# Attention products of two chunks in one run, and two output products in shared PSUM banks

## The chip, the cores and the metric

The kernel runs on one core of one Trainium2 chip. The metric is the device time of one execution in microseconds (us), lower is better. The engines that matter here are TensorE (PE, matrix products; its weight loads are shown as PEld), VectorE (DVE), ScalarE (ACT) and GpSimd (POOL); SyncE (SP) issues most of the transfers. Products are written into PSUM, which has eight banks of 512 float32 columns on 128 partitions; PE writes it, DVE and ACT read it.

## What is computed

One transformer block in float32: causal attention with rotary positions (4 sequences of 1024 tokens, width 256, 16 heads of 64), a residual and a layer norm, then a mixture of experts (16 experts, the best 3 for each token), a residual and a layer norm. The change lies in attention alone:

```python
proj = x @ W_in.T + b_in
...
q = _rope(q, sin, cos)
k = _rope(k, sin, cos)
att = jnp.einsum('bhqd,bhkd->bhqk', q, k) * scale
att = jnp.where(mask, att, -jnp.inf)
att = jax.nn.softmax(att, axis=-1)
y = jnp.einsum('bhqk,bhkd->bhqd', att, v)
y = y.transpose(0, 2, 1, 3).reshape(b, t, H * VD)
return y @ W_out.T + b_out
```

## The kernel before

Attention works on pairs of heads: 8 pairs for each of the 4 sequences, `n` from 0 to 31. A sequence is cut into 8 chunks of 128 tokens. Each pair is worked through in six slots, `k` from 0 to 5 (the loop from L535), and the pairs are a pipeline: while the scores of pair `n` are made, the rest of pair `n - 1` is finished and the queries and keys of pair `n + 1` are projected. The order of instructions on PE and DVE is the order in which the code stands; it is written out by hand (`manual_schedule`).

Slot by slot, on PE, for a pair `n` in the middle:

- slot 0: scores of query chunk 7; output product 3 of pair `n - 2`; a key projection; products of key chunks 4 and 3 of pair `n - 1`
- slot 1: scores of chunk 6; a key projection; products 2 and 1 of pair `n - 1`
- slot 2: scores of chunk 5; a query projection; product 0 of pair `n - 1`, then `close(n - 1)`
- slot 3: scores of chunk 4; product 7 of pair `n`; output product 0 of pair `n - 1`; a value projection
- slot 4: scores of chunks 3 and 2; product 6 of pair `n`; output product 1 of pair `n - 1`; a value projection
- slot 5: scores of chunks 1 and 0; a query projection; output product 2 of pair `n - 1`; product 5 of pair `n`

`scores` (L393) multiplies queries by keys, DVE masks and reduces the result to its row minimum (L401), ACT takes the exponential (L416), POOL divides by the row sum (L433), and two slots later DVE transposes the probabilities in 32x32 blocks into `t_last` and `t_first` (`turn`, L452).

`product(n, j)` (L459 to L485) multiplies the transposed probabilities of key chunk `j` by the values of that chunk. Chunk `j` matters to query chunks `j` to 7 alone, so low chunks have wide products. Each product has 32 rows and 64 columns of weights, so PE is cut into eight positions: four row groups `a` (0 to 3) times two column halves `hh`, one for each head. There are four products `u` for each position. Some of them are of a kind that the mask cuts by 32 columns more (`skip`): for an odd chunk those with `u < a`, for an even chunk those with `u > a`. Odd chunks have thus more work in row group 0, even ones in row group 3. In chunk 7 the cut products are empty and left out: 20 products, ordered by row group, in place of 32. All products of a pair add up in four PSUM tiles `y`, one for each row group, of which the first 256 of 512 columns are used. The pool `ps_y` has those four buffers, so product 7 of a pair can write a tile when `close` of the pair before has copied it.

`close(n)` (L487) has ACT copy the four tiles, with the bias of the values, into `yT` in SBUF. `out(n, h)` (L500) multiplies a quarter of `yT`, as weights, by the output weights (two products, L503), into a buffer of the pool `ps_s`, and DVE adds the result to the residual (L590).

The pool `ps_s` has the other four PSUM banks. The scores, projections, value products and output products take its buffers in turn; each waits until what was last in the buffer has been read by DVE or ACT.

DVE also takes router work of the batch before into its idle times (`fill`), so that later pairs have more of it than the first eight. After the last pair two more turns of the loop finish what is left, and the mixture of experts follows (L1054 to L1121).

Of the kernel before, what the change touches and what calls it, by code (L numbers as in the profile page):

```python
# [29 lines left out]
FP = mybir.dt.float32  # L30
I32 = mybir.dt.int32
AF = mybir.ActivationFunctionType
ALU = mybir.AluOpType
AX = mybir.AxisListType
PSUM = bass.MemoryType.PSUM
# [3 lines left out]
P = 128  # L39
B, T, D = 4, 1024, 256  # L40
H, KD = 16, 64
# [3 lines left out]
TC = T // P  # L45
# [74 lines left out]
def attention(  # L120
# [6 lines left out]
    nc = tc.nc  # L127
    with ExitStack() as ctx:
        def pool(name, bufs, **kw):
            return ctx.enter_context(tc.tile_pool(name=name, bufs=bufs, **kw))  # L130
# [13 lines left out]
        sp = pool("a_small", 4)  # L144

        ps_s = pool("ps_s", 4, space=PSUM)
        ps_y = pool("ps_y", 4, space=PSUM)

        xT_v = xT.rearrange("b (c p) t -> b p c t", p=P)
        x_v = x.rearrange("b (c p) d -> b p c d", p=P)  # L150
# [291 lines left out]
        turned = {}  # L442
# [11 lines left out]
                probs[n, i, hh][:, ds(512 * h, n_j * P)].rearrange("p (j u q) -> p u j q", u=4, q=32),  # L454
            ), kind)

        st = {}

        def product(n, j):  # L459


            if j == TC - 1:
                st[n] = [ps_y.tile([P, 512], FP, tag="y", name="y_ps") for _ in range(4)]
            h, jh = divmod(j, 4)
            t, c = turned[n][h], jh // 2
            v, c = (vrs[n, h, c], 0) if h else (vrs[n, h, None], c)
            at = jh * (8 - 4 * h)
            us = range(4) if 0 < j < TC - 1 else range(3, -1, -1)
            parts = [(u, hh, a) for u in us for hh in range(2) for a in range(4)]

            def whole(u, a):
                return u >= a if j % 2 else u <= a

            if j == TC - 1:

                parts = sorted((p for p in parts if whole(p[0], p[2])), key=lambda p: -min(3 - p[2], 2))
            for u, hh, a in parts:
                skip = 0 if whole(u, a) else 1
                nc.tensor.matmul(  # L479
                    st[n][a][ts(hh, KD), ds(32 * (j + skip), 32 * (TC - j - skip))],  # L480
                    lhsT=v[ts(a, 32), c * 8 + 2 * u + jh % 2, ts(hh, KD)],
                    rhs=t[ts(a, 32), hh, u, ds(at + skip, TC - j - skip), :],
                    start=(j == TC - 1 and u == 3), stop=(j == 0 and u == 0),
                    skip_group_check=True,
                )  # L485

        def close(n):  # L487
            p = n % NP
            yT = yp.tile([P, TC, 4, 32], FP, tag="yT")
            y = st.pop(n)  # L490
            for a in reversed(range(4)):

                y_copied = nc.scalar.activation(  # L493
                    yT[:, :, a, :], y[a][:, : 2 * P].rearrange("p (i q) -> p i q", q=32),
                    AF.Identity, bias=bv[:, p : p + 1],
                )
            st[n] = yT.rearrange("p i a q -> p (i a q)")
            router.closed = y_copied

        def out(n, h):  # L500
            ps = ps_s.tile([P, 2, D], FP, tag="s", name="oo")
            for v in range(2):
                nc.tensor.matmul(  # L503
                    ps[:, v, :], lhsT=st[n][:, ts(2 * h + v, P)], rhs=wo[n],
                    start=True, stop=True,
                )
            return accs[n // NP][:, ds(2 * h, 2), :D], ps

# [25 lines left out]
        with tc.manual_schedule(engines={mybir.EngineType.PE, mybir.EngineType.DVE}):  # L534
            for n in range(n_pairs + 2):  # L535
# [3 lines left out]
                for k in range(n_slots):  # L539
# [32 lines left out]
                    if k == 2 and before:  # L572
                        product(n - 1, 0)
                        close(n - 1)
                    if k in (3, 4) and here:
                        product(n, 10 - k)
                    if k in (0, 3, 4, 5) and one_of(n - 1 - (k == 0)):
                        part = out(n - 1 - (k == 0), (k - 3) % 4 if k else 3)
                    if k in (3, 5):
# [44 lines left out]
                    if k == 0 and one_of(n):  # L624
                        rotate(n, 0, 0)
                    if k < 2 and before:
                        product(n - 1, 4 - 2 * k)
                        product(n - 1, 3 - 2 * k)
                    m = n + 2 - n % 2
                    if k in (3, 4) and one_of(m):  # L630
                        values(m, 2 * (n % 2) + k - 3)
# [736 lines left out]
```

## Time and profile before

| what | value |
|---|---|
| time, median of 3 runs | 1563.44 us (1563.33 to 1567.95) |
| the profiled execution, its own time | 1566.73 us |
| its span, first to last instruction | 1565.0 us |
| mean granted TensorE clock | 0.986 |
| attention, first to last product (L479) | 40.0 to 1125.9 us |
| a pair of heads, most of them | 33.60 us |
| matmuls of `product` (L479), `t_first` and `t_last` | 8192 and 7424 |
| matmuls of `out` (L503) | 512 |
| ACT's copies in `close` (L493) | 128, median 476 ns |
| DVE's sums after `out` (L590) | 128, mean 659 ns |

A float32 product is recorded as two matmuls, each with its weight load. A line of the timeline has the start in us, the time from the first start to the last end, the engine, line, operation, what is written and read, the tile on PE, the shape and the count; idle time before it and what ended it stand in brackets. Matmuls overlap: the end of a line is modelled and lies behind the start of the next, so a step's cost is read from start to start.

### The profile page before, as it was taken

How to read it: one execution, taken by the hardware profiler on the slowest of the kernel's cores; microseconds unless marked ns; L12 is line 12 of the kernel's file. 1: busy time of each engine (PE TensorE's matmuls, PEld its weight loads, DVE VectorE, ACT ScalarE, POOL GpSimd, SP SyncE). 2: the span in 40 equal slices, each digit the busy share in tenths (PEclk: the TensorE clock that was granted, in tenths of full speed). 3: DMA queues.
4: the chain of work that ended last, by engine and by line, in shares of the span. 5: the costliest groups of instructions: out<-in, count | busy, mean ns of one | idle time of the engine just before them, and what ended most of it. 6: DMA issues, size and time to landing. Idle time of an engine off the chain costs nothing.

```text
span 1565.0 us, 52508 instructions
## 1 busy us (share of the span) xinstructions
PE 1502.5 (96%) x20844; PEld 1051.4 (67%) x20844; DVE 1173.4 (75%) x3677; ACT 730.7 (47%) x1695; POOL 979.7 (63%) x932
## 2 busy tenths in 40 slices
PE   8999999999999999999999999999899999999990
PEld 4566666666666666666665666665588888888880
DVE  4788888898899999988999999889857333333334
ACT  3555555557555555664554556654342222222224
POOL 3676565676556667776776667767457764444444
PEclk9999999999999999999999999999999999999995
DMA  6554545546454554564546445645488998888868
GB/s 187 142 151 128 147 119 138 165 119 187 110 145 120 138 160 113 155 182 135 162 134 168 125 124 144 187 127 138 151 311 259 374 307 227 257 255 258 259 131 328
DMA packets 120473, 280.34 MB, mean 179 GB/s; under 512 B 21392, under 2 KB 64656, under 8 KB 108688
## 3 DMA queue, kind: packets, MB, share of 16 engines
q1 hardware_dynamic: 100304, 250.05, 53.1%
q0 software_dynamic: 19584, 26.62, 8.1%
q8 instruction: 166, 2.72, 0.7%
q14 instruction: 83, 0.68, 0.1%
q10 hardware_dynamic: 336, 0.27, 0.1%
HBM read 186.81 MB, written 61.09 MB: 158 GB/s over the span
## 4 chain that ended last, share of the span: by engine, by line
PE 89%; DVE 6%; DMA 2%; issue 2%; ACT 1%; SPq 0%; POOL 0%; ACTq 0%; DVEq 0%; POOLq 0%
PE y_ps L479 18%; PE s L393 17%; PE pp L290 14%; PE ps L1106 11%; PE ps L1090 11%; PE oo L503 7%; PE vv L343 7%; PE ps L1054 1%; DVE p L401 1%; DVE t_first L452 1%; PE lg_ps L723 1%; DMA vr<-v_d 1%; DVE o_stats L1226 1%; DMA more<-sums 0%; PE x_ps L715 0%
## 5 line engine op out<-in xcount | busy, mean ns | idle before, releaser
L433 POOL TENSOR_SCALAR p<-p,rinv 128x512 f32<-128x512 f32 (+7 forms) x512 | 374.8, 747 | 340.6 <-DVE rinv L430 310.3
L416 ACT ACTIVATE p<-p,nmax 128x512 f32<-128x512 f32 (+7 forms) x512 | 391.7, 766 | 412.6 <-DVE nmax L401 322.4
L393 PE MATMUL s<-rotk,rotq 64*128 64x512 f32 (+3 forms) x1536 | 310.9, 514 | 4.0 <-DVE rotk L326 2.7
L452 DVE STREAM_TRANSPOSE t_first<-p 128x512 f32<-128x512 f32 (+3 forms) x512 | 275.9, 582 | 8.6 <-PE y_ps L479 8.4
L1121 POOL DMA_INDIRECT sums<-y,ids x104 | 163.1, 1569 | 162.1 <-DVE y L1117 126.3
L290 PE MATMUL pp<-xT,wqk 128*128 128x512 f32 x512 | 250.9, 613 | 3.0 <-DVE nmax L401 3.0
L1095 ACT ACTIVATE hid<-ps,w 128x256 f32<-128x256 f32 (+1 forms) x224 | 89.7, 456 | 289.8 <-issue 237.7
L479 PE MATMUL y_ps<-t_first,vr 32*64 32x224 f32 (+3 forms) x8192 | 208.7, 331 | 6.9 <-issue 2.7
L393 PEld LDWEIGHTS s<-rotk,rotq 64*128 64x128 f32 x1536 | 139.0, 187 | 100.8 <-issue 56.5
L479 PEld LDWEIGHTS y_ps<-t_first,vr 32*64 32x64 f32 x8192 | 168.9, 131 | 55.4 <-issue 47.5
L1111 DVE TENSOR_TENSOR y<-ps,w 128x512 f32<-128x512 f32 (+1 forms) x56 | 36.6, 653 | 215.8 <-PE ps L1106 192.5
L1090 PE MATMUL ps<-xg,w 128*128 128x256 f32 (+1 forms) x896 | 189.5, 364 | 1.3 <-DVE xg L1057 0.7
L1106 PE MATMUL ps<-w,hid 128*128 128x256 f32 x832 | 188.8, 379 | 0.5 <-ACT hid L1095 0.5
L401 DVE CUSTOM_DVE_ANT_0 p<-s,zero_and_mask,nmax 128x512 f32<-128x512 f32 x256 | 181.8, 748 | 2.9 <-PE s L393 0.7
L401 DVE CUSTOM_DVE_ANT_0 p<-s,mask 128x512 f32<-128x512 f32 (+1 forms) x256 | 131.8, 552 | 62.9 <-PE s L393 62.8
L1106 PEld LDWEIGHTS ps<-w,hid 128*128 128x128 f32 x832 | 157.2, 190 | 21.6 <-ACT hid L1095 0.7
L290 PEld LDWEIGHTS pp<-xT,wqk 128*128 128x128 f32 x512 | 89.9, 190 | 119.7 <-issue 63.2
L1090 PEld LDWEIGHTS ps<-xg,w 128*128 128x128 f32 x896 | 157.2, 190 | 19.2 <-DVE xg L1057 1.0
L479 PEld LDWEIGHTS y_ps<-t_last,vr 32*64 32x64 f32 x7424 | 104.9, 131 | 76.5 <-issue 49.8
L503 PE MATMUL oo<-wo,yT 128*128 128x256 f32 x512 | 141.0, 398 | 2.9 <-ACT yT L493 1.6
L479 PE MATMUL y_ps<-t_last,vr 32*64 32x32 f32 (+3 forms) x7424 | 126.8, 243 | 0.5 <-DVE t_last L452 0.4
L820 POOL DMA_INDIRECT xs<-acc,slots x96 | 97.3, 1014 | 44.3 <-issue 21.2
(190 smaller groups left out, 1833.9 us busy)
## 6 DMA issues: line engine op xcount, KB each, us to landing
w<-in_wall_dram SPq DMA_DIRECT2D x56, 1154.0 KB
vr<-v_d SPq DMA_DIRECT2D x256, 128.0 KB
vr<-v_d SPq DMA_DIRECT2D x128, 256.0 KB
swq<-rawq SPq DMA_DIRECT2D x256, 64.0 KB
v_d<-v SPq DMA_DIRECT2D x128, 128.0 KB
swk<-rawk SPq DMA_DIRECT2D x124, 128.0 KB
x<-xs SPq DMA_DIRECT2D x48, 264.0 KB
wqk<-in_w_qk_dram SPq DMA_DIRECT2D x32, 256.0 KB
```

Of the source, the lines that this page charges most:

```text
L290: nc.tensor.matmul(ps, lhsT=wqk[n][:, c, i, :], rhs=xts[b, g][:, c, :], start=(c == 0), stop=(c == DC - 1),)
L343: nc.tensor.matmul(ps[:, u, :], lhsT=xts[b, cc // 2][:, c, ts(cc % 2 * 2 + u, P)], rhs=wv[n][:, c, :], start=(c == 0), stop=(c == DC - 1),)
L393: nc.tensor.matmul(s[:, :n_k], lhsT=rot[n, 0, qc // 4][ts(hh, KD), ts(qc % 4, P)], rhs=k[ts(hh, KD), ds(k0, n_k)], start=True, stop=True,)
L401: i = nc.vector.tensor_tensor_reduce(out=probs[n, qc, hh][:, ds(k0, n_k)], in0=s[:, :n_k], in1=masks[qc % 2][:, 512 - n_k :] if diag else ...
L416: order["exp"] = nc.scalar.activation(pr, pr, AF.Exp, bias=m, scale=-1.0, accum_out=rsum[:, hh : hh + 1])
L433: order["divide"] = router.behind = nc.gpsimd.tensor_scalar(pr, pr, rinv[:, hh : hh + 1], 1.0, ALU.mult, ALU.mult)
L452: order["turn"] = router.on_dve = after(nc.vector.transpose(turned[n][h][:, hh, :, ds(i - 4 * h, n_j, step=7 - 4 * h), :], probs[n, i, hh] ...
L479: nc.tensor.matmul(st[n][a][ts(hh, KD), ds(32 * (j + skip), 32 * (TC - j - skip))], lhsT=v[ts(a, 32), c * 8 + 2 * u + jh % 2, ts(hh, KD)], ...
L503: nc.tensor.matmul(ps[:, v, :], lhsT=st[n][:, ts(2 * h + v, P)], rhs=wo[n], start=True, stop=True,)
L1090: nc.tensor.matmul(ps[:, f - f0, :], lhsT=w[:, ds(c * FF + f * P, P)], rhs=xg[:, c, :n], start=(c == 0), stop=(c == DC - 1),)
L1106: nc.tensor.matmul(ps[:, h, :], lhsT=hid[:, f, ts(h, P)], rhs=w[:, ds(W2_AT + f * D, D)], start=(f == 0), stop=(f == FC - 1),)
L1121: s = behind(nc.gpsimd.indirect_dma_start(out=sums_of(t), out_offset=bass.IndirectOffsetOnAxis(ap=ids[:, h : h + 1], axis=0), in_=y[:, h, ...
```

## The change

Four things change.

1. The four PSUM tiles of `product` become one tile of four banks, `[P, 4, 512]`, in a pool with one buffer. Product 7 of a pair therefore starts when everything that reads the tile of the pair before is done.
2. `product` takes several chunks at once and puts their products into one order: each position's products are numbered by the columns that the position has been sent before, and all are sorted by that number. Chunks 7 and 6 are now one such run in slot 4 (slot 3 has no product any more), 4 and 3 are one in slot 0, 2 and 1 one in slot 1. Chunks 5 and 0 stay alone, but are sorted too.
3. Output products 0 and 1 go into the unused columns 256 to 511 of the banks of the product tile: output 0 of pair `n - 1` into banks 0 and 1 of its own tile, in slot 3, output 1 of pair `n - 1` into banks 2 and 3 of the tile of pair `n`, in slot 4 after the run of chunks 7 and 6. They are written without the flag that begins an accumulation (`start=False`). Outputs 2 and 3 stay in `ps_s`.
4. In the last pair two of the four copies of `close` are made by DVE.

```diff
-        ps_y = pool("ps_y", 4, space=PSUM)
+        ps_y = pool("ps_y", 1, space=PSUM)
...
+        def product(n, *js):
+
+            if js[0] == TC - 1:
+                st[n] = banks["y"] = ps_y.tile([P, 4, 512], FP, tag="y", name="y_ps")
+            todo, moved = [], {}
+            for j in js:
+                first_last = j in (0, TC - 1)
+                for u in range(3, -1, -1) if first_last else range(4):
+                    for hh in range(2):
+                        for a in range(4):
+                            skip = u < a if j % 2 else u > a
+                            if skip and j == TC - 1:
+                                continue
+                            at = moved.get((hh, a), 0)
+                            moved[hh, a] = at + TC - j - skip
+                            todo.append((at if j < TC - 1 else -min(3 - a, 2), j, u, hh, a, int(skip)))
+            for _, j, u, hh, a, skip in sorted(todo, key=lambda i: i[0]):
...
                 nc.tensor.matmul(
-                    st[n][a][ts(hh, KD), ds(32 * (j + skip), 32 * (TC - j - skip))],
+                    st[n][ts(hh, KD), a, ds(32 * (j + skip), 32 * (TC - j - skip))],
...
+                from_y = y[:, a, : 2 * P].rearrange("p (i q) -> p i q", q=32)
+                if n == n_pairs - 1 and a % 2:
+                    nc.vector.tensor_scalar(
+                        yT[:, :, a, :], from_y, bv[:, p : p + 1], 1.0, ALU.add, ALU.mult
+                    )
+                else:
+                    y_copied = nc.scalar.activation(
+                        yT[:, :, a, :], from_y, AF.Identity, bias=bv[:, p : p + 1],
+                    )
...
         def out(n, h):
-            ps = ps_s.tile([P, 2, D], FP, tag="s", name="oo")
+            apart = h == 0 or (h == 1 and n + 1 < n_pairs)
+            if apart:
+                ps = banks["y"][:, ds(2 * h, 2), D:]
+            else:
+                ps = ps_s.tile([P, 2, D], FP, tag="s", name="oo")
             for v in range(2):
                 nc.tensor.matmul(
                     ps[:, v, :], lhsT=st[n][:, ts(2 * h + v, P)], rhs=wo[n],
-                    start=True, stop=True,
+                    start=not apart, stop=True, skip_group_check=apart,
                 )
...
-                    if k in (3, 4) and here:
-                        product(n, 10 - k)
+                    if k == 4 and here:
+                        product(n, 7, 6)
...
                     if k < 2 and before:
-                        product(n - 1, 4 - 2 * k)
-                        product(n - 1, 3 - 2 * k)
+                        product(n - 1, 4 - 2 * k, 3 - 2 * k)
```

More of the change, by code (lines that the diff above doesn't have):

```diff
@@ L455, in turn @@
             ), kind)
[L457 to L478, printed above, removed]
+        st, banks = {}, {}
@@ new lines, in product @@
+        def product(n, *js):
[14 more added lines that the diff above has]
+            for _, j, u, hh, a, skip in sorted(todo, key=lambda i: i[0]):
+                h, jh = divmod(j, 4)
+                t, c = turned[n][h], jh // 2
+                v, c = (vrs[n, h, c], 0) if h else (vrs[n, h, None], c)
@@ L479, in product @@
                 nc.tensor.matmul(
-                    st[n][a][ts(hh, KD), ds(32 * (j + skip), 32 * (TC - j - skip))],
+                    st[n][ts(hh, KD), a, ds(32 * (j + skip), 32 * (TC - j - skip))],
                     lhsT=v[ts(a, 32), c * 8 + 2 * u + jh % 2, ts(hh, KD)],
-                    rhs=t[ts(a, 32), hh, u, ds(at + skip, TC - j - skip), :],
+                    rhs=t[ts(a, 32), hh, u, ds(jh * (8 - 4 * h) + skip, TC - j - skip), :],
                     start=(j == TC - 1 and u == 3), stop=(j == 0 and u == 0),
@@ L491, in close @@
             for a in reversed(range(4)):
[L493 to L496, printed above, removed]
+                from_y = y[:, a, : 2 * P].rearrange("p (i q) -> p i q", q=32)
[7 more added lines that the diff above has]
+                    )
             st[n] = yT.rearrange("p i a q -> p (i a q)")
```

## The prediction

> **What bounds the kernel now.** I read the page first. TensorE (PE) has work in flight for 96% of the span, and nine tenths of the chain that ended last are PE.
>
> ```profile
> PE 1502.5 (96%) x20844; PEld 1051.4 (67%) x20844; DVE 1173.4 (75%) x3677; ACT 730.7 (47%) x1695; POOL 979.7 (63%) x932
> ...
> PE 89%; DVE 6%; DMA 2%; issue 2%; ACT 1%; SPq 0%; POOL 0%; ACTq 0%; DVEq 0%; POOLq 0%
> ...
> L503 PE MATMUL oo<-wo,yT 128*128 128x256 f32 x512 | 141.0, 398 | 2.9 <-ACT yT L493 1.6 <-DVE nmax L401 1.0
> ```
>
> So only what shortens PE's own row of work counts. The output products (L503) lose 2.9 us in all to waits: there is next to nothing to win by giving them other buffers.
>
> Then the timeline of PE over one pair of heads (start, duration, engine, line). A step's cost is the start of the next line minus its own.
>
> ```profile
> 174.27 1.45 PE L393 MATMUL s<-rotk,rotq 64*128 64x128 f32 x8
> 175.65 0.73 PE L479 MATMUL y_ps<-t_last,vr 32*64 32x32 f32 x40
> 176.31 1.13 PE L503 MATMUL oo<-wo,yT 128*128 128x256 f32 x4
> 177.28 1.89 PE L343 MATMUL vv<-wv,xT 128*128 128x256 f32 x8
> 179.10 1.77 PE L393 MATMUL s<-rotk,rotq 64*128 64x512 f32 x8
> 180.80 0.93 PE L479 MATMUL y_ps<-t_last,vr 32*64 32x64 f32 x64
> 181.66 1.13 PE L503 MATMUL oo<-wo,yT 128*128 128x256 f32 x4
> ...
> 188.08 1.05 PE L479 MATMUL y_ps<-t_last,vr 32*64 32x96 f32 x64
> 189.05 1.99 PE L393 MATMUL s<-rotk,rotq 64*128 64x512 f32 x8
> ...
> 199.60 2.97 PE L479 MATMUL y_ps<-t_first,vr 32*64 32x192 f32 x128
> 202.50 1.56 PE L393 MATMUL s<-rotk,rotq 64*128 64x256 f32 x8
> 203.99 1.98 PE L290 MATMUL pp<-xT,wqk 128*128 128x512 f32 x4
> 205.91 1.98 PE L479 MATMUL y_ps<-t_first,vr 32*64 32x224 f32 x64
> ```
>
> Chunk 7's product costs 0.66 (slot 3), chunk 6's 0.86 here and 0.90 in most pairs (slot 4), chunk 5's 0.97, 4 with 3 2.18 (193.80 to 195.99 of the same timeline), 2 with 1 2.90, chunk 0's 1.91. Such a pair lasts 33.60 us, and most of the 31 do: VectorE (DVE) is busy for 87% of it in the first batch and up to 96% later, which PE hides.
>
> The next timeline shows what chunk 7's product hides in slot 3 of the following pair.
>
> ```profile
> 207.82 1.45 PE L393 MATMUL s<-rotk,rotq 64*128 64x128 f32 x8
> 208.00 1.56 ACT L493 ACTIVATE yT<-y_ps,bv 128x256 f32<-128x256 f32 x4
> 209.20 0.73 PE L479 MATMUL y_ps<-t_last,vr 32*64 32x32 f32 x40
> 209.86 1.13 PE L503 MATMUL oo<-wo,yT 128*128 128x256 f32 x4
> ```
>
> The output product needs all four copies of yT, which end at 209.56. PE spends the time till then on the scores and on chunk 7.
>
> **Slot 3 loses chunk 7's product.** Its output product would follow the scores at 209.20, but waits for yT: 209.56 + 0.05 (at the end of attention yT ends at 1127.51 and the output starts at 1127.56) = 209.61 in place of 209.86. Of the 0.66 us that leave, 0.25 are won; the other 0.41 had been free cover. Bounds: 0.66 if the copies came sooner, 0 if the output came no sooner; both ends of the wait are rows, so I take -0.25.
>
> **Slot 4 gets 52 products for 32.** No row has the merged run. The nearest is chunk 6's, whose 0.86 us I cut into windows (start:end, length, then busy time and count of what is in work, matmuls first, weight loads second):
>
> ```profile
> 180.80:181.08 0.28, 0.28 (x32) 0.28 (x33) 1.00 0.26 69
> 181.08:181.15 0.07, 0.07 (x31) 0.07 (x12) 1.00 0.12 29
> 181.15:181.48 0.33, 0.33 (x51) 0.33 (x33) 1.00 0.29 31
> 181.48:181.66 0.18, 0.18 (x24) 0.11 (x9) 1.00 0.10 28
> ```
>
> The first 16 products (32 matmuls, a product being two) are issued within 0.28 us, the other 16 in the next 0.40, and the last 0.18 passes to the next step with few loads left. After the first 16 a product costs 0.40/16 = 25 ns: 0.28 + 36 x 0.025 + 0.18 = 1.36 us. Below: all at the first pace, 0.28/16 = 17.5 ns, gives 1.09. Above: the two rows' sum, 0.66 + 0.90 = 1.56. I take 1.36, against 0.90 so far: +0.46 (+0.19 to +0.66).
>
> **The order inside the runs.** PE has eight positions (four row groups by two column halves). Before, each round of eight gives the odd chunks' extra 32 columns to one group and the even chunks' to another; now a product goes where the fewest columns have been sent. Chunk 0's run shows what a column costs where nothing is uneven: its busiest position takes 4 products of 256 columns, 32 blocks of 32. A block is 0.053 us: in the run of chunks 4 and 3 a position's 128-column matmuls, each half of four blocks, follow each other by 0.107 us. So 32 are 1.71 of its 1.91: entry and exit are 0.20. Chunks 4 and 3 give each position 33 blocks: 1.76 + 0.20 = 1.96 against 2.18; 2 and 1 give 49: 2.61 + 0.20 = 2.81 against 2.90. At most 0.22 + 0.09 = 0.31 is there; nothing at all if PE's queue already evens it out. Wide blocks (2, 1) are near chunk 0's row, so most of 0.09; narrow ones (4, 3) are nearer to chunk 5's, whose 12 blocks should take 0.84 and take 0.97 for want of issue: I take half of each, -0.15. Chunks 5 and 0 keep their heaviest position: 0, within 0.03.
>
> **The banks.** The outputs of slots 3 and 4 no longer take a buffer from the scores' four; that wait was 26.8 us of idle weight loads but 1.0 of matmuls: 0. In return PE gets waits. The merged run's first matmul now waits for the sum of slot 3 (DVE, old L590), and behind it in PE's queue stand the whole run, an output and a value projection, for which ACT's copy waits. In the timeline of DVE that sum ends at 179.09, the run's place is 180.80: 1.7 us to spare (1.57 at the least in full pairs). Chunk 5's product waits for the sum of slot 4, which ends at 183.78, against 188.08. Cost 0; beyond that slack each us late is lost in each pair. The sums stay where they are in DVE's order, no DMA and no step of POOL moves.
>
> [...] If each of the two waits exposed its sum of 0.65 us, 24 pairs would lose 31 us; by the slack above they lose none. [...]
>
> **The last close** is split between ACT and DVE: four copies took 1.57 us at 1125.94 with nothing beside them. Two take about half, and DVE, which idles then, does the others: -0.7 (0 to -0.8).
>
> **The sum.** A pair changes by -0.25 + 0.46 - 0.15 = +0.06. Six pairs (from 515, 550, 652, 826, 930 and 965 us on) wait for DVE in slots 1 and 2, together some 7 us over 2.90 and 1.49, and swallow either sign; the last pair is DVE's too. So 24 x 0.06 = +1.4; the first pair has no output in slot 3: 1.36 for 0.62 + 0.84, -0.1; the end -0.7. Total +0.6. The profiled execution took 1566.7 around a span of 1565.0, the median of the runs is 1563.4; on that median I predict **1564.0 us**.
>
> **Rivals.** About 0.3% (4.7 us) is what a measurement of this kernel tells from no change; below, "same" means within it.
> - *Slower: the merged run is no cheaper than its two rows.* It is long enough to live on the slow pace, and nothing but its own rate sets it. For: chunk 6's row falls from 17.5 to 25 ns a product after 16. Against: one entry and exit are saved. At 1.56 the pair changes by +0.26: 24 x 0.26 - 0.8 = +5.4, 1568.9; if the order also brings nothing, +0.41 x 24 - 0.8 = +9, 1572.5. With the order's 0.15 it decides from 1.53 us a run.
> - *Faster: evenness was the limit.* Both sorted runs fall to their columns and the merged one keeps the first pace: -0.25 + 0.19 - 0.31 = -0.37, 24 times and -0.8: 1553.8. For: 0.22 of excess in chunks 4 and 3. Against: chunk 5's excess, which no order removes. Half of it gives 1558.2, about the border.
> - *It frees buffers, and that is what counts:* the 7 us in the six pairs go, 1557. Against: those waits are two slots away from the outputs that move, for turns and reductions of DVE, whose work stays.
> - *It doesn't do what it says:* the runs stay apart. The built order shows 52 products in one run, so no chance.
>
> **How the numbers follow.** Forecast 0.55, own range 1559 to 1568. Slower 0.25, faster by evenness 0.15, by buffers 0.05. Range with both sides, cut where 0.2 is left out: **1555 to 1571**. Faster 0.20, same 0.55, slower 0.25.
>
> **What would show it.** Slot 3's output starts at yT's end + 0.05, some 0.4 us after the scores would let it; the merged run of 104 matmuls lasts 1.36; 4 with 3 falls to about 2.07, 2 with 1 to 2.85; a full pair lasts 33.5 to 33.8; the end of attention has two copies a side. I am wrong if the merged run starts late (the sum of DVE), if it is under 1.2 or over 1.5, or if pairs that wait for DVE change.

## The result, and the profile after

The changed kernel takes 1568.96 us (median of 20 runs, 1565.89 to 1572.57), the kernel before, run beside it, 1564.48 us (20 runs, 1562.27 to 1567.95): ratio 1.0028, 95% interval 1.0021 to 1.0035. It is slower by about 4.5 us, just inside the 0.3% that the prediction counted as no change; 1564.0 had been forecast, with a range of 1555 to 1571.

The page of the changed kernel begins as that of before, but its chain of work that ended last is another:

```profile
PE 1491.7 (95%) x20844; PEld 1045.0 (67%) x20844; DVE 1175.4 (75%) x3679; ACT 730.0 (47%) x1693; POOL 979.8 (63%) x932
...
PE 75%; DVE 11%; ACT 5%; issue 4%; DMA 3%; SPq 1%; POOL 1%; ACTq 0%; POOLq 0%; DVEq 0%
```

PE is busy for 10.8 us less (1502.5 before), and yet the span is longer: what was saved on PE came back as waiting. The chain, nine tenths PE before, now leaves it in every pair. The timeline of PE over one pair shows where (start, duration, engine, line, operation; idle time before it and what ended it in brackets; start to start is a step's cost):

```profile
203.94 1.45 PE L393 MATMUL s<-rotk,rotq 64*128 64x128 f32 x8
205.73 1.13 PE L512 MATMUL y_ps<-wo,yT 128*128 128x256 f32 x4 [0.34 <-ACT yT L499]
206.70 1.89 PE L343 MATMUL vv<-wv,xT 128*128 128x256 f32 x8
208.52 1.77 PE L393 MATMUL s<-rotk,rotq 64*128 64x512 f32 x8
210.22 1.42 PE L479 MATMUL y_ps<-t_last,vr 32*64 32x32 f32 x104
211.57 1.13 PE L512 MATMUL y_ps<-wo,yT 128*128 128x256 f32 x4
...
223.71 1.10 PE L479 MATMUL y_ps<-t_last,vr 32*64 32x128 f32 x61
...
225.85 1.77 PE L393 MATMUL s<-rotk,rotq 64*128 64x384 f32 x8
...
229.47 2.91 PE L479 MATMUL y_ps<-t_first,vr 32*64 32x192 f32 x128
232.30 1.56 PE L393 MATMUL s<-rotk,rotq 64*128 64x256 f32 x8
```

Slot 3: the output (L512) starts 1.79 after the scores, and 0.34 of that is a wait for `yT`. Before, chunk 7's product stood there and the output came after 2.04. So 0.25 is won for 0.66 of work taken away. Slot 4: the run of chunks 7 and 6, 104 matmuls, takes 1.35 (210.22 to 211.57) for chunk 6's 0.90. Slot 0, chunks 4 and 3: 2.14 (2.18 before). Slot 1, chunks 2 and 1: 2.83 here, 2.84 in most pairs (2.90). The next line, of ScalarE, has the copies that slot 3 waits for; they end at 205.67, and the output starts 0.06 later.

```profile
204.11 1.56 ACT L499 ACTIVATE yT<-y_ps,bv 128x256 f32<-128x256 f32 x4
```

At the end of attention there is one surprise. The timeline of all engines there:

```profile
1124.70 0.48 DVE L495 TENSOR_SCALAR yT<-y_ps,bv 128x256 f32<-128x256 f32 x1 [3.14 <-PE y_ps L479]
1125.22 0.47 ACT L499 ACTIVATE yT<-y_ps,bv 128x256 f32<-128x256 f32 x1 [10.08 <-DVE yT L495]
1125.73 0.48 DVE L495 TENSOR_SCALAR yT<-y_ps,bv 128x256 f32<-128x256 f32 x1 [0.54 <-ACT yT L499]
1126.24 0.47 ACT L499 ACTIVATE yT<-y_ps,bv 128x256 f32<-128x256 f32 x1 [0.55 <-DVE yT L495]
...
1126.77 1.39 PE L512 MATMUL y_ps<-wo,yT 128*128 128x256 f32 x4 [2.11 <-ACT yT L499]
```

The two engines do not share the work, they take turns: each copy waits for the one before it on the other engine, 0.52 a turn, and the output comes 2.07 after the first copy. In the kernel before, ScalarE alone started its copies at 1125.94 and the output came at 1127.56, after 1.62.

Where the time of the two profiled executions went, worked out from the start of the first copy of each `close` (in the changed kernel's last one that is VectorE's, at 1124.70):

| stretch | before, us | after, us | difference |
|---|---|---|---|
| to the first close | 73.64 | 69.37 | -4.27 |
| the 19 full pairs, mean of one | 33.61 | 33.70 | +0.09 each, +1.7 |
| the ten longer pairs, sum | 360.47 | 361.73 | +1.26 |
| the last two periods | 53.23 | 53.30 | +0.07 |
| last close to the end | 439.02 | 441.91 | +2.89 |
| span | 1565.0 | 1566.6 | +1.6 |

A full pair is one of the usual length; in the kernel before it waits for nothing but PE, in the changed one also for `yT`. The first row says nothing of the change: in the profiles of the experiments below that keep the merged run it reads from 69.45 to 75.38. Without it the stretches make +5.9, and the medians +4.5.

### The profile page after: what moved, and what is told of

Same layout as the page of the kernel before. It is cut to its first block, busy times and chain, and to the rows that moved or that the text cites. A ratio compares the mean times of both kernels' runs of the same rounds, so it can differ in the third digit from the quotient of the medians.

```text
span 1566.6 us, 52499 instructions
## 1 busy us (share of the span) xinstructions
PE 1491.7 (95%) x20844; PEld 1045.0 (67%) x20844; DVE 1175.4 (75%) x3679; ACT 730.0 (47%) x1693; POOL 979.8 (63%) x932
## 3 DMA queue, kind: packets, MB, share of 16 engines
q8 instruction: 166, 2.72, 0.7%
## 4 chain that ended last, share of the span: by engine, by line
PE 75%; DVE 11%; ACT 5%; issue 4%; DMA 3%; SPq 1%; POOL 1%; ACTq 0%; POOLq 0%; DVEq 0%
PE s L393 13%; PE y_ps L479 13%; PE ps L1114 11%; PE ps L1098 11%; PE pp L290 9%; PE vv L343 7%; PE y_ps L512 4%; PE oo L512 3%; ACT yT L499 3%; DVE t_last L452 2%; DVE p L401 2%; PE ps L1062 1%; DVE rotq L295 1%; ACT rawq L301 1%; DVE t_first L452 1%
## 5 line engine op out<-in xcount | busy, mean ns | idle before, releaser
L479 PE MATMUL y_ps<-t_first,vr 32*64 32x224 f32 (+3 forms) x8192 | 204.8, 331 | 4.2 <-DVE t_first L452 2.2
L1098 PE MATMUL ps<-xg,w 128*128 128x256 f32 (+1 forms) x896 | 189.5, 365 | 1.7 <-DVE xg L1065 1.7
L401 DVE CUSTOM_DVE_ANT_0 p<-s,zero_and_mask,nmax 128x512 f32<-128x512 f32 x256 | 181.7, 747 | 2.8 <-PE s L393 0.7
L401 DVE CUSTOM_DVE_ANT_0 p<-s,mask 128x512 f32<-128x512 f32 (+1 forms) x256 | 131.3, 550 | 65.6 <-PE s L393 65.5
L1098 PEld LDWEIGHTS ps<-xg,w 128*128 128x128 f32 x896 | 157.2, 190 | 19.5 <-DVE xg L1065 2.1
L479 PEld LDWEIGHTS y_ps<-t_last,vr 32*64 32x64 f32 x7424 | 100.7, 131 | 53.5 <-issue 26.1
L343 PE MATMUL vv<-wv,xT 128*128 128x256 f32 x512 | 121.3, 380 | 0.9 <-issue 0.9
L479 PE MATMUL y_ps<-t_last,vr 32*64 32x32 f32 (+3 forms) x7424 | 118.1, 244 | 1.8 <-DVE acc L599 1.2
```

Of the source, the lines that this page charges most:

```text
L343: nc.tensor.matmul(ps[:, u, :], lhsT=xts[b, cc // 2][:, c, ts(cc % 2 * 2 + u, P)], rhs=wv[n][:, c, :], start=(c == 0), stop=(c == DC - 1),)
L401: i = nc.vector.tensor_tensor_reduce(out=probs[n, qc, hh][:, ds(k0, n_k)], in0=s[:, :n_k], in1=masks[qc % 2][:, 512 - n_k :] if diag else ...
L479: nc.tensor.matmul(st[n][ts(hh, KD), a, ds(32 * (j + skip), 32 * (TC - j - skip))], lhsT=v[ts(a, 32), c * 8 + 2 * u + jh % 2, ts(hh, KD)], ...
L1098: nc.tensor.matmul(ps[:, f - f0, :], lhsT=w[:, ds(c * FF + f * P, P)], rhs=xg[:, c, :n], start=(c == 0), stop=(c == DC - 1),)
```

## The experiments

All ratios are to the kernel before, run on the same chip in the same rounds; the changed kernel stands at 1.0028 (1.0021 to 1.0035).

### The order alone

The kernel before, with sorted runs; chunks 7 and 6 stay apart, with four PSUM tiles:

```diff
-                        product(n - 1, 4 - 2 * k)
-                        product(n - 1, 3 - 2 * k)
+                        product(n - 1, 4 - 2 * k, 3 - 2 * k)
...
+            for _, j, u, hh, a, skip in sorted(todo, key=lambda i: i[0]):
```

> The kernel before with one edit: the products of chunks 4 and 3, of 2 and 1, of 5 and of 0 are put in the order of columns sent so far, as in the changed kernel; chunks 7 and 6 stay apart in slots 3 and 4, four PSUM tiles, outputs in ps_s, the last close on ScalarE. Theory (what the changed kernel's rows show): the order is worth 0.04 us in the run of 4 and 3 and 0.06 in that of 2 and 1, so these read 2.14 and 2.84 here too, a pair lasts 33.50, and 24 to 31 such pairs give -2.4 to -3.1 us: about 1561.5 beside 1564.5, ratio 0.998 to 0.9985. Rival A: those gains come from the one tile (one release in place of four), not from the order: the rows stay at 2.18 and 2.90, ratio 1.000. Rival B: the prediction's own size, -0.15 a pair: ratio 0.997 or below.

Measured: ratio 0.9986 (0.9976 to 0.9995). 4 with 3 takes 2.14 and 2 with 1 2.84, a full pair 33.50: the rows of the changed kernel, without its one tile. Rival A falls. The order is worth 0.10 a pair, two thirds of the 0.15 predicted. Slot 3 of this kernel shows the cover that the changed one has given away: chunk 7's product stands between scores and output, and nothing waits.

```profile
173.12 1.45 PE L393 MATMUL s<-rotk,rotq 64*128 64x128 f32 x8
174.50 0.73 PE L479 MATMUL y_ps<-t_last,vr 32*64 32x32 f32 x40
175.16 1.13 PE L503 MATMUL oo<-wo,yT 128*128 128x256 f32 x4
```

### The changed kernel without the order

```diff
-            for _, j, u, hh, a, skip in sorted(todo, key=lambda i: i[0]):
+            for _, j, u, hh, a, skip in sorted(todo, key=lambda i: (-i[1], i[0] if i[1] == TC - 1 else 0)):
```

> The changed kernel with the order taken out: chunk 7's products, then chunk 6's in plain rounds, in one run; 4 then 3 and 2 then 1 in plain rounds as before. Theory: 4 with 3 goes back to 2.18, 2 with 1 to 2.90 (+0.10 a pair), and the merged run goes from 1.34 to about 1.40, since its length is set by the number of products (25 ns each past the first 16): together +0.10 to +0.16 a pair, 2.5 to 5 us more than the changed kernel, ratio to the kernel before 1.0045 to 1.006. Rival: the order is what made the merged run cheap, without it the run costs the two rows' sum of 1.56 (+0.32 a pair, 8 to 10 us more than the changed kernel, ratio 1.008 to 1.009).

Measured: ratio 1.0047 (1.0034 to 1.006). A full pair takes 33.82, 0.13 more than the changed kernel's 33.69: 0.05 in the run of 4 and 3 (2.19), 0.06 in that of 2 and 1 (2.90), and 0.02 to 0.03 in the merged run (timeline of PE; 177.55 to 178.92, 1.37):

```profile
177.55 1.44 PE L479 MATMUL y_ps<-t_last,vr 32*64 32x32 f32 x104
178.92 1.13 PE L512 MATMUL y_ps<-wo,yT 128*128 128x256 f32 x4
```

So merging alone made the run cheaper than the two rows' sum of 1.56, and the order made little of it. The rival falls.

### Chunk 7's products by columns sent

In the changed kernel chunk 7's products keep the order by row group that they had when each group's tile came free by itself. Here they are numbered like all others:

```diff
-                            todo.append((at if j < TC - 1 else -min(3 - a, 2), j, u, hh, a, int(skip)))
+                            todo.append((at, j, u, hh, a, int(skip)))
```

> The changed kernel with chunk 7's 20 products numbered by columns sent, like all others, and not by their row group in three steps (a relic of the time when each group's tile came free by itself). Theory: the merged run is a matter of how even the eight positions are served as much as of its 52 products; it gets shorter by about 0.1 us, 1.34 to 1.25: a full pair 33.59, -2.5 to -3 us against the changed kernel, ratio to the kernel before 1.001. Rival: 25 ns a product rule the run (as the prediction had it), the order does nothing: 1.34, 33.68, ratio 1.0028.

Measured: ratio 1.0016 (1.0007 to 1.0025). The merged run takes 1.28 in the pair shown (timeline of PE) and 1.28 to 1.31 in most, and a full pair 33.62, 0.07 less:

```profile
178.44 1.36 PE L479 MATMUL y_ps<-t_last,vr 32*64 32x32 f32 x104
179.72 1.13 PE L512 MATMUL y_ps<-wo,yT 128*128 128x256 f32 x4
```

Evenness counts in the merged run too, by some 0.06 of the 0.1 that the theory gave it. 25 ns a product is a good measure of an uneven run, not a floor.

### Outputs 0 and 1 back in the shared buffers

```diff
-            apart = h == 0 or (h == 1 and n + 1 < n_pairs)
+            apart = False
```

> The changed kernel with output products 0 and 1 back in buffers of ps_s (with the flag that begins an accumulation); the merged run and the one tile stay. Theory: the banks are worth nothing in either sense: a full pair 33.69 as in the changed kernel, total within 1 us of it (ratio 1.0025 to 1.003); only the merged run of the last two pairs, which waited 0.4 and 0.6 us for VectorE's sum, starts without a wait. Rival A: the shared buffers cost waits (scores wait for the sums): more than 0.1 us a pair, +3 us or more. Rival B: the sums that now stand between the pairs' products (merged run and chunk 5 wait for them) are what the changed kernel lost: -3 us or more.

Measured: ratio 1.005 (1.0037 to 1.0063). The theory falls: the idle halves of the banks are worth something. In the first eight pairs nothing changes, 33.68. In many pairs of the later batches the output of slot 3 comes 1.96 after the scores, not 1.79, and the pair takes 33.82. The timelines of PE and of VectorE in one of them:

```profile
759.96 1.46 PE L393 MATMUL s<-rotk,rotq 64*128 64x128 f32 x8
761.92 1.10 PE L512 MATMUL oo<-wo,yT 128*128 128x256 f32 x4 [0.51 <-ACT yT L499]
```

```profile
760.28 1.29 DVE L452 STREAM_TRANSPOSE t_first<-p 128x512 f32<-128x512 f32 x2
761.50 0.12 DVE L430 RECIPROCAL rinv<-rsum 128x2 f32<-128x2 f32 x1
761.54 0.27 DVE L401 CUSTOM_DVE_ANT_0 p<-s,zero_and_mask 128x128 f32<-128x128 f32 x1
761.74 0.09 DVE L401 DVE_READ_ACCUMULATOR2_ANT nmax<- 128x1 f32 x1
```

PE's bracket names `yT`, but the copies had ended at 761.70, and the output should have started at 761.76. What came last was VectorE, whose first reduction of the scores, late behind router work, ended at 761.81 and, by these times, set the buffer free. So rival A holds in kind, with 0.14 us in such pairs. They make up only part of the 3.4 us by which the ratios differ; one pair (965 us) was 1.4 longer in this profile and the last one 2.2, in which the granted clock was 0.50 to 0.64 from 1108 to 1116 us, after an idle time of 1.93.

### The last close on ScalarE alone

```diff
-                if n == n_pairs - 1 and a % 2:
-                    nc.vector.tensor_scalar(...)
-                else:
-                    y_copied = nc.scalar.activation(...)
+                y_copied = nc.scalar.activation(...)
```

> The changed kernel with all four copies of the last close on ScalarE, as before. Theory: the split close is the loss: VectorE and ScalarE took turns, 2.02 us where ScalarE alone takes 1.57, and the slower granted clock that follows (0.79) follows from it too: the last output products wait 1.6 us and run at full clock again, 0.5 to 1.9 us less than the changed kernel. Rival A: the low clock at the end has another cause (it stays at 0.79 here): only the 0.45 comes back. Rival B: the split gains after all, as the prediction had it: 0.7 us more than the changed kernel. A time of the whole cannot tell 0.5 us; the rows of the last close and the clock of the twelve output products after it (2.75 us at full clock, 3.80 at 0.79) do.

Measured: ratio 1.002 (1.0011 to 1.003), 0.0008 below the changed kernel's, though the two intervals overlap. The windows around the last close, of the changed kernel first, then of this one (start:end, length, busy time and count of PE, PEld, DVE, ACT, POOL, then the granted clock, DMA share and GB/s):

```profile
1124.70:1126.80 2.10, 0.03 (x1) 0.03 (x1) 0.96 (x2) 0.95 (x2) 0.00 (x0) 1.00 0.00 0
1126.80:1129.00 2.20, 2.20 (x9) 2.03 (x10) 0.69 (x1) 0.00 (x0) 0.00 (x0) 0.66 0.48 120
1129.00:1132.50 3.50, 3.50 (x14) 2.83 (x13) 2.51 (x8) 0.43 (x2) 0.00 (x0) 0.73 0.93 304
```

```profile
1125.70:1127.30 1.60, 0.00 (x0) 0.00 (x0) 0.00 (x0) 1.57 (x4) 0.00 (x0) 1.00 0.00 0
1127.30:1129.00 1.70, 1.66 (x10) 1.53 (x11) 0.07 (x1) 0.05 (x1) 0.00 (x0) 1.00 0.34 51
1129.00:1132.00 3.00, 3.00 (x19) 2.66 (x18) 2.93 (x9) 0.38 (x2) 0.00 (x0) 1.00 0.94 295
```

The turns cost 0.45 directly (2.07 against 1.62), and PE then runs at 0.66 and 0.73 of its clock, the twelve output matmuls in 3.80 in place of 2.76. With ScalarE alone the clock stays at 1.00 through these windows; it falls to 0.50 for 3.4 us only from 1135.3 on, after another idle time, of 1.95. The other profiles show nearly the same contrast: of the six kernels with this alternating split five have 0.52 to 0.66 in the 2 to 3 us after it (one, with the projection in a buffer of `ps_s`, 1.00), and the seven without alternating copies, the kernel before among them, all have 1.00. Counted from the first copy, the experts' first product (L1098, here L1093) starts after 10.21 in the changed kernel and after 8.61 in this one: in these two profiles the split close lost about 1.6 us where the prediction had it win 0.7.

### The last close split by halves of the queries

To find what makes the engines take turns: ScalarE copies the first half of the queries of all four banks into one tile, VectorE the second half into another.

```diff
+                lo, hi = yT[:, :4], yp.tile([P, TC, 4, 32], FP, tag="yT", name="yT")[:, :4]
+                for a in reversed(range(4)):
...
+                    y_copied = nc.scalar.activation(
+                        lo[:, :, a, :], from_y[:, :4], AF.Identity, bias=bv[:, p : p + 1],
+                    )
+                    nc.vector.tensor_scalar(
+                        hi[:, :, a, :], from_y[:, 4:], bv[:, p : p + 1], 1.0, ALU.add, ALU.mult
+                    )
```

> The changed kernel with the last close split in another way: ScalarE copies the first half of the queries of all four banks into one tile, VectorE the second half into another tile (before: two whole banks each, into interleaved columns of one tile). Theory: the two engines took turns in the changed kernel because they wrote interleaved parts of one tile and each write waited for the one before; with a tile for each they work side by side: four copies of half the width on each, 0.3 us each, about 1.2 us and 0.35 to 0.45 less than ScalarE alone, 0.8 less than the changed kernel: ratio 1.002. Rival: the turns come from the banks, which both read: then eight short copies in turn, 2.2 us or more, and nothing is won: ratio 1.0028.

Measured: ratio 1.0038 (1.002 to 1.0057), on a chip where the kernel before took 1582.83 us. The theory falls: eight copies in turn, 3.17 from the first to the output (timeline of all engines).

```profile
1140.69 0.37 ACT L495 ACTIVATE yT<-y_ps,bv 128x128 f32<-128x128 f32 x1 [8.41 <-PE y_ps L479]
1141.09 0.35 DVE L498 TENSOR_SCALAR yT<-y_ps,bv 128x128 f32<-128x128 f32 x1 [2.38 <-ACT yT L495]
1141.47 0.37 ACT L495 ACTIVATE yT<-y_ps,bv 128x128 f32<-128x128 f32 x1 [0.42 <-DVE yT L498]
```

A tile of its own for each writer does not help. In the brackets each of these copies after the first waits for the one before it on the other engine (0.42 to 0.44 each from the third on), and in the trace of the changed kernel the three later copies carry a semaphore wait for the other engine's copy: it is the program that makes them take turns; what they still share is the PSUM tile that they read, and in it the same bank.

### The last close with nothing shared

The sorted kernel, in which each bank is a tile of its own. ScalarE copies banks 3 and 2 into one tile, VectorE banks 1 and 0 into another; the outputs of the last pair become two products of 64 rows in place of one of 128.

```diff
+                for a in (3, 1, 2, 0):
...
+                    if a < 2:
+                        nc.vector.tensor_scalar(
+                            lo[:, :, a, :], from_y, bv[:, p : p + 1], 1.0, ALU.add, ALU.mult
+                        )
+                    else:
+                        y_copied = nc.scalar.activation(
+                            hi[:, :, a - 2, :], from_y, AF.Identity, bias=bv[:, p : p + 1],
+                        )
```

> The sorted kernel (four PSUM tiles, order alone) with the last close split so that nothing is shared: ScalarE copies banks 3 and 2 into one tile, VectorE banks 1 and 0 into another. The output products of the last pair become two of 64 rows each in place of one of 128, 16 more matmuls, which add up to 1.9 us at the very end if they run one after the other and little if the two column halves run side by side; so the time of the whole says nothing here, the rows of the close do. Theory: the engines took turns because the program made them: the four banks were one tile, and the copies of two engines from one tile wait for each other. With a tile for each bank they run side by side: from the first copy to the output 1.05 us (two copies of 0.48 and the way to TensorE) in place of 1.57 to 1.65, which is what the prediction reckoned for the changed kernel. Rival: two engines reading PSUM at once slow each other: copies of 0.7 us or more, 1.5 and up.

Measured: ratio 0.9979 (0.997 to 0.9988), 1561.60 us beside 1565.61: the lowest ratio of the study, though the order alone (0.9986) lies within its interval. The timeline of all engines:

```profile
1122.26 0.88 DVE L497 TENSOR_SCALAR yT<-y_ps,bv 128x256 f32<-128x256 f32 x2 [3.30 <-PE y_ps L479]
1122.32 0.84 ACT L501 ACTIVATE yT<-y_ps,bv 128x256 f32<-128x256 f32 x2 [9.78 <-PE y_ps L479]
...
1123.19 1.10 PE L521 MATMUL oo<-wo,yT 128*64 128x256 f32 x8 [0.85 <-DVE yT L497]
```

Both engines copy at once, at the pace of one alone (two copies in 0.88 and 0.84; ScalarE alone took 1.57 for four), and the output starts 0.93 after the first copy: 0.69 less than the 1.62 of ScalarE alone. In this run the two engines read different banks and did not slow each other. In the changed kernel their banks differed too, and they took turns of 0.52: by these two runs the limit there was the program's wait, not the memory. What made it wait is not told apart further: in the changed kernel the engines shared the PSUM tile and `yT`, in the split by halves the PSUM tile and each bank, here none of them.

### Slot 3: the value projection ahead of the output

Does any work fill the 0.34 in slot 3? First with the projection's result in the idle halves of banks 0 and 1, so that it needs no buffer of `ps_s`:

```diff
+                    if k == 3 and one_of(mv):
+                        values(mv, 2 * (n % 2), "y" in banks)
                     if k in (0, 3, 4, 5) and one_of(n - 1 - (k == 0)):
...
+            if apart:
+                ps = banks["y"][:, :2, D:]
```

> The changed kernel with slot 3 in another order on TensorE: scores, value projection, output product 0 (before: scores, output, value projection). So that the projection needs no buffer of ps_s, its result goes into the idle halves of banks 0 and 1 of the product tile, and output 0 into ps_s. Theory: in slot 3 TensorE does nothing for 0.34 us in every pair because the output needs the four copies of yT; the projection needs none of them, fills the hole, and by the time it ends (1.8 us) yT is there: a full pair goes from 33.68 to 33.34, 28 to 30 pairs give -9 to -10 us against the changed kernel: about 1559, ratio to the kernel before 0.9965. Rival A: VectorE gets the output's result 1.5 us later, its sum delays the score reductions behind it, and the merged run, which waits for the projection's copy on ScalarE, starts late: half of it or nothing, ratio 1.000 to 1.003. Rival B: the hole is not made by yT but by something that the scores need: the projection starts no sooner, ratio 1.0028.

Measured: ratio 1.002 (1.0008 to 1.0033); a full pair 33.68, unchanged. The projection starts 1.79 after the scores, as the output did, and its bracket names the copies whose result it does not read:

```profile
206.27 1.45 PE L396 MATMUL s<-rotk,rotq 64*128 64x128 f32 x8
208.06 1.99 PE L346 MATMUL y_ps<-wv,xT 128*128 128x256 f32 x8 [0.34 <-ACT yT L502]
```

It writes the tile that ScalarE still reads, and starts 0.06 after the copies end (at 208.00). So what was put into the product tile waited for `yT` too, and the experiment could not fill the hole. Of its rivals B comes nearest: what gates the step is the copies, but through the tile.

Then with the projection in a buffer of `ps_s`:

> The same order in slot 3 (scores, value projection, output), but with the buffers of the changed kernel: the projection takes one of the four buffers of ps_s, which the four score tiles before it fill. Theory: the first of them is read by VectorE's first two reductions, which end about 0.2 us after the scores' last product starts to drain: the projection starts 0.2 to 0.3 us late in the first eight pairs and later where VectorE is full: 0.0 to -0.15 us a pair, 0 to -4 us against the changed kernel, ratio 1.000 to 1.003. Rival: score buffers are no limit, -0.34 a pair as in the run with the bank halves: ratio 0.9965.

Measured: ratio 1.0007 (0.9998 to 1.0016). A full pair takes 33.60 to 33.64 in the first six pairs and 33.81 in most later ones. In the first batch the projection starts 1.71 after the scores, `[0.26 <-DVE nmax L401]`, later 1.92: the four score tiles fill the four buffers, and it waits for VectorE's first reduction. 0.08 is won where VectorE is early, 0.13 lost where it is not. These rows don't explain the ratio, which lies 3.3 us below the changed kernel's with intervals that don't meet. In the two profiles 2.8 of the 3.1 us between the spans lie behind the last close (439.15 and 441.91), after which the clock stayed at 1.00 here, though the close takes its 2.07 in turns as before. Whether that holds in every run isn't shown.

### Output 3 of the pair before moved into slot 3

```diff
+                    moved = n < n_pairs and not (p == 1 and b)
+                    if k == (3 if moved else 0) and one_of(n - 2):
+                        parts.append(out(n - 2, 3, moved))
+                    if k in (3, 4, 5) and before:
+                        parts.append(out(n - 1, k - 3))
```

> The changed kernel with three edits: (1) output product 3 of pair n - 2, which stood in slot 0, now stands in slot 3 ahead of output 0 of pair n - 1, so that something that needs neither yT nor a buffer of ps_s lies between the scores and output 0; it goes into the idle halves of banks 2 and 3 (output 1 goes back to ps_s, the output weights are loaded in slot 4); (2) chunk 7's products by columns sent; (3) the last close on ScalarE alone. Theory: TensorE's 0.34 us in slot 3 are a hole that any work of at least that length fills if it needs no score buffer; banks 2 and 3 are copied first, so that output 3 can start 0.3 us or more before output 0 could. Full pair 33.62 (measured with edit 2 alone) less 0.34: 33.28, against 33.60 of the kernel before; 26 pairs, -8 us and the end's -1 against the changed kernel with edit 2: 1556 to 1558, ratio to the kernel before 0.995. Rival A: the wait moves on: with nothing after the scores of slot 0, a projection there waits for a score buffer as long, 33.60. Rival B: the second sum of VectorE in slot 3 makes the merged run late, 33.5 to 33.6 in the later batches: ratio 0.998 to 1.000.

Measured: ratio 1.0072 (1.0046 to 1.0098), on the chip where the kernel before took 1582.83 us. It failed twice over. Output 3, into banks 2 and 3, which are copied first, still came 1.79 after the scores (at 238.42 here) with the 0.34 for `yT`: again the whole tile (timeline of PE; the line holds outputs 3 and 0):

```profile
240.21 1.99 PE L507 MATMUL y_ps<-wo,yT 128*128 128x256 f32 x8 [0.34 <-ACT yT L494]
```
And with no output in slot 0 the run of chunks 4 and 3 there takes 2.52 in place of 2.14, and a full pair 34.0: a wait moved on, as rival A had it, though to another place. What that run waits for the profile does not name.

### Three edits together

The projection ahead of the output (in the banks), chunk 7 by columns, the close on ScalarE:

> The changed kernel with three edits together: the value projection ahead of the output in slot 3 (result in the bank halves), chunk 7's products by columns sent, the last close on ScalarE alone. Theory: they add up: 33.68 - 0.34 - 0.09 = 33.25 a full pair, and 0.5 to 1 us at the end: -12 to -14 us against the changed kernel, about 1556, ratio to the kernel before 0.994. Rival: VectorE, busy for 87 to 96 per cent of a pair, becomes the bound before that, first in the pairs of the later batches: 33.6 there and 33.25 in the first eight, ratio 0.998.

Measured: ratio 0.9997 (0.9988 to 1.0006). A full pair takes 33.58: chunk 7's order gives 0.10, the projection nothing, as alone. Theory and rival both fall with the first edit. It is level with the kernel before, as the rows say: 33.58 and 33.60.

### A merge that gives away no copies' cover

The sorted kernel with chunk 5 taken out of slot 5 and joined to 4 and 3:

```diff
-                    if k == 5 and here:
-                        product(n, 5)
...
-                        product(n - 1, 4 - 2 * k, 3 - 2 * k)
+                        product(n - 1, *((5, 4, 3), (2, 1))[k])
```

> The kernel before, sorted (as in the run with the order alone: chunk 7 in slot 3, chunk 6 in slot 4, four tiles), with one edit more: chunk 5's product leaves slot 5 and joins 4 and 3 in slot 0, one run of 192 matmul pairs' worth of three chunks. Theory: a merged run saves its entry and exit (about 0.2) and some unevenness, as the run of 7 and 6 did (1.28 for 0.66 + 0.90 where fully sorted); what cost the changed kernel that gain was that chunk 7 had been cover for yT's copies. Chunk 5 stands between an output and the scores of the next slot and covers no copies, so the gain should stay: 2.9 in place of 0.98 + 2.14, a full pair 33.50 less 0.2 to 0.3 = 33.2 to 33.3, -6 to -9 us against the sorted kernel, ratio to the kernel before 0.993 to 0.995. Rival A: chunk 5 covers something after all: the scores of slot 0 follow those of slot 5 sooner and wait for buffers that VectorE has not read: 33.5 or more, ratio 0.9986 and up. Rival B: a long run has no entry and exit to save (25 ns a product from the first): 33.45 to 33.5.

Measured: ratio 1.034 (1.0321 to 1.0359), 1619.43 us beside 1565.61, the slowest of the study. Rival A holds, in the timeline of PE:

```profile
262.32 2.16 PE L393 MATMUL s<-rotk,rotq 64*128 64x512 f32 x8
265.27 1.13 PE L503 MATMUL oo<-wo,yT 128*128 128x256 f32 x4 [0.79 <-DVE nmax L401]
```

Chunk 5 did cover something: without it the output of slot 0 comes 2.95 after the scores, not 1.97, because it waits for a score buffer. The run itself, where undisturbed, takes 2.96 to 3.02 against 3.12 apart: 0.1 to 0.16 saved for 0.98 of cover lost, 34.25 the shortest full pair. Most pairs are far longer, for another reason:

```profile
196.17 0.95 PE L479 MATMUL y_ps<-t_first,vr 32*64 32x128 f32 x37
200.10 1.34 PE L479 MATMUL y_ps<-t_first,vr 32*64 32x160 f32 x24 [2.98 <-issue]
201.37 2.83 PE L393 MATMUL s<-rotk,rotq 64*128 64x384 f32 x8
```

In the midst of the run PE stands still for 2.98 us, for nothing that the profile names (the last section has more on it), and the scores after it, at a granted clock of 0.50, take 2.76 in place of 1.70. Such a period lasts up to 42.5.

## Why the prediction was right, and where its sizes were off

**Right: slot 3.** Predicted -0.25, for an output that would start at the end of `yT` + 0.05; measured -0.25, at + 0.06. The order-alone kernel, with chunk 7 still in its place, waits for nothing there.

**Right: the merged run.** Predicted 1.36, measured 1.34 to 1.35. The kernel without the order shows 1.37, so the first rival (no cheaper than 1.56) was wrong about merging itself. The rate behind the 1.36, 25 ns a product, belongs to an uneven run: sorted fully it takes 1.28 to 1.31, and 1.25 with the three edits together. That the sum met the number is in part luck, since it took the run's length for a matter of its count of products alone.

**Mis-sized: the order.** Predicted -0.15 (to 2.07 and 2.85), measured -0.10 (2.14 and 2.84). The wide run fell as reckoned, the narrow one by 0.04 in place of 0.11. Taken alone it gives 33.50 from 33.60, taken out 33.82 from 33.69. A full pair thus changed by +0.09, not +0.06.

**Wrong sign: the last close.** Predicted -0.7 (0 to -0.8), measured +0.45, and a slower clock behind it that the prediction had not thought of; putting the copies back on ScalarE moves the ratio from 1.0028 to 1.002, within the intervals, and the experts' first product by 1.6 us. The step that failed is "Two take about half, and DVE, which idles then, does the others": it priced the copies and not the waits between them. With nothing shared the same split gives -0.69.

**Partly wrong: the covers.** The slacks of 1.7 and 4.3 us for the new waits held in all pairs but the last two, where the merged run waited 0.39 and 0.62 us for VectorE's sum (no value projection stands ahead of it there); those two periods are longer by 0.07 in all, so these waits cost next to nothing. Of the six pairs that were to "swallow either sign" four came out 0.10 to 0.25 longer and two 0.16 and 0.99 shorter, -0.37 together. The other four of the ten longer pairs are 1.63 longer, 1.25 of it in the one from 376 us (373 in the changed kernel) on, in which PE stood still for 0.86 us for "issue".

**Right for a reason that had gone: the banks.** Cost 0 was right for the change as made. But the row it came from, 1.0 us of waits, was measured with chunk 7's product in front of the output. With that cover gone the buffer is late by 0.17 in many later pairs, and the idle bank halves save it.

**Rows that the sum did not use.** In the timeline of PE before, a projection with scores in front of it takes 1.91 ahead of a product (197.69 to 199.60) and 1.82 ahead of an output (185.30 to 187.12). A third takes 1.81 ahead of the run of 4 and 3 (191.99 to 193.80), with an output in front of it in place of scores. The three rows fit a cost of some 0.1 for each change of tile shape, in front or behind; by that estimate from three rows a run less between scores and output would save 0.1. No run measures it apart.

Together: 19 full pairs +1.7, the longer ones +1.3, the last two +0.1, the end +2.9, against +1.4, 0, 0 and -0.7 predicted. Most of the miss is the last close and what comes after it. The stretch from there to the end also holds the experts' part, and varies: 438.7 to 440.2 us in five profiles with the last close on ScalarE alone, 439.2 to 442.0 in the six with the alternating split (two more were taken on the slower chip). So the time lies inside the range though the sum was +0.6 and the medians differ by 4.5: the pairs brought +3.1 for +1.4, the end +2.9 for -0.7.

## What to carry to other kernels

Before a short step is moved or merged, look at what it covers on the other engines: chunk 7's 0.66 us were worth only 0.25 where they stood, chunk 5's 0.98 came back whole as a wait when they left, and merging saved 0.1 to 0.3. One tile made of several PSUM banks was also one unit of waiting here: a product into an idle half waited 0.34 us for the readers of all four banks, in two experiments. Copies by two engines went in turn wherever they shared a PSUM tile (2.07 from the first to the output with four copies, 3.17 with eight), and side by side where they shared nothing (0.93). An order that evens out the positions of PE cost nothing here and kept its gain alone, 0.10 a pair; try the parts of such a change one by one, since the sum here hid a gain (0.9986) behind two losses.

## What the runs showed of the hardware that was not expected

In these profiles PE's granted clock fell to 0.50 after idle times of 1.4 to 3 us: in the changed kernel for 3.4 us after the 2.11 at the last close (1127.5 to 1130.9 us; the 0.66 there is the mean of a window that starts before the fall), in the chunk 5 run after 2.98 (0.50 from 201 to 203 us), and in the run with outputs 0 and 1 back in the shared buffers after 1.93 (0.64 from 1108 to 1112 us and 0.50 from 1112 to 1116, which makes some 6.9 us). Right after the 1.5 to 1.7 of a close on ScalarE alone it was 1.00 in all six profiles. Idle length alone does not settle it: one of the six gaps of 2.1 us at the last close was followed by 1.00, while in the run with the projection in the banks a gap of 1.45 us was followed by 0.50 (662 to 665 us). The 1.36 us that PE waits for VectorE in the last pair were followed by 0.50 in the changed kernel (1117.3 to 1120.6 us) and by 1.00 in the kernel before (1117 to 1120 us). What else decides is not shown.

In long runs of small matmuls PE stopped for "issue", for up to 4.4 us in the chunk 5 run. One queue of instruction transfers moves 166 packets of 16 KB, 2.72 MB. If all of it is PE's, that is some 65 bytes for each of its 41,688 matmuls and weight loads, so that, by this estimate, the 384 of the run of three chunks use one and a half packets within 3 us. In the trace's DMA records a packet on that queue starts at 197.41 us, while PE stands still from 197.1 to 200.1, at the end of a stretch in which the DMA engines were busy for 92 to 100% with other loads. The packet took until 198.68, and PE went on 1.42 later. All twelve such stops of 0.7 us or more in this profile's attention end 1.24 to 1.67 us after a packet of that queue has ended, and so do the 22 in the other thirteen profiles (1.20 to 1.72): by these times what PE waited for were its instructions. That the packet came late because of the other loads is argued, not shown. All stalls of this kind make 28 us there, and 1.7 us in the changed kernel. Behind the five of 2.1 us and more in the chunk 5 run the clock was at 0.50 for 27 us in all.

In the last pair of the kernel whose last close shares nothing, 24 matmuls of 64 columns, two halves of PE side by side, took 2.81 us, the same as 12 of 128 columns (2.76): the doubled count that had been feared cost nothing.
